# Attention and feed-forward block on one core: the value products of a unit gathered into one run, with new constants in the planner

## The chip, the cores and the metric

One NeuronCore of a Trainium2 chip runs the whole kernel. The metric is the device time of one execution in microseconds (us), lower is better. Before the change the median of three runs is 1599.75 us (1596.24 to 1602.34).

## The reference, cut to what matters

A transformer block on x of 2 x 1024 x 512 in float32: layer norm with a shift and a scale from a small vector, attention (32 query heads, 8 key heads, 64 wide, rotary positions, causal), a gated residual, a second layer norm, a feed-forward part with ternary weights (groups of 64), and a gated residual. The part that the change touches is this:

```
scores = jnp.einsum('bhqd,bhkd->bhqk', q, k) / jnp.sqrt(jnp.float32(D))
scores = jnp.where(causal[None, None], scores, jnp.finfo(x.dtype).min)
attn = jax.nn.softmax(scores, axis=-1)
out = jnp.einsum('bhqk,bhkd->bhqd', attn, v)
```

## The kernel before, in words

The kernel has four stages in time: projections of q, k and v (in the profiled execution up to about 316 us), attention (the first scores at 317 us, the last row sums end at 1050 us), the product with Wo together with the second norm (from 1039 us), and the feed-forward part (from 1232 us to the end).

**Units.** Attention is cut into 64 units: 2 batches, 8 key heads, and 4 groups of 256 queries, each for the 4 query heads of a key head. A unit of group i has 2, 4, 6 or 8 key blocks of 128 keys (nb = 2 * i + 2). The groups come in the order 2, 4, 6, 8, except in the last key head of the last batch, where it is reversed. So there are 16 rounds of four units with 20 blocks each.

**What a unit does.** Tiles are named as in the profile.

- Tops. To have a value to subtract in the softmax, TensorE first multiplies queries and keys once in a single pass, queries on the partitions: `pm`, two matmuls at a time on two 64-row halves of the array, each into a PSUM bank of its own. VectorE reduces each `pm` to a maximum per query: `mm` by a plain reduction, `junk` (followed by a read of the accumulator, `mx`) by a reduction with the causal mask. 48 such reductions belong to a round. The maxima are turned (`mt`) and go by DMA into a row (`row`).
- Scores. For each key block TensorE makes exact scores with keys on the partitions, from high and low parts, and subtracts the row of maxima: tiles `ps_`, two PSUM banks for a chain of blocks. Within a chain the next block is accumulated onto the banks of the block before, after ScalarE has read that with its exponentials (`e`, two of 128x512 for a block).
- Values. `value(j)` multiplies a block's exponentials with the values, `po`, on two 64-column halves of the array, in one PSUM bank for the whole unit. The bank is claimed by the first value task and freed when ScalarE has copied `po` out (`on`).
- Sums. GpSimd, and VectorE for block 1, add the exponentials (`acc`); TensorE sums them over the keys with ones (`pr`, four 32-column quarters). The inverse goes through DRAM and comes back as `ri`; GpSimd multiplies `on` with it.

Beside attention runs the rounding of the feed-forward weights, 48 tiles of 128x512: three ScalarE steps, one matmul (`pq`) and six VectorE steps (`ws`, `wm_`, `wr`). The first TBEFORE = 20 of them are due within attention.

**What sets the order.** Every task of attention and of what follows is added to a planner (class Plan) with an engine, a cost, a due time and what it needs. `Plan.run` keeps a modelled clock and takes tasks one by one; the order in which it takes them is the order in each engine's queue, since every engine is kept in program order. A PSUM tile (tag "#") gets the bank that is free first by the model. For TensorE the choice is in lines 129 to 133: of the tasks that can start within TURN, the one with the least due time, corrected by STICK (a bonus for the mode that the array is in), LATE (a penalty for a task that becomes ready only just then), and BOOST or DELAY for the tops, which feed VectorE, by how much VectorE work is `behind` (BOOST below FEED). A move out of mode 3 (tops and scores) is put off for a top while less than FILL is behind:

```
best = min((o for o in opts if o[0] <= start + TURN),
           key=lambda o: (o[2].due - STICK * (CLASS[o[2].mode] == CLASS[mode]) + LATE * o[1] - (o[2].feeds > 0) * (BOOST * (behind < FEED) - DELAY * (behind > ENOUGH)), o[2].n))
if mode == 3 and best[2].mode != 3 and behind < FILL:
    best = min((o for o in opts if o[0] <= start + TURN and o[2].feeds > 0), key=lambda o: (o[2].due, o[2].n), default=best)
```

The modes are ways of cutting the array: 0 whole, 1 the values, 2 the row sums, 3 tops and scores. The values of a unit become tasks of SPAN[nb] blocks each (lines 974 to 982); a value task is one uninterrupted stretch of TensorE's queue:

```
if (at + 1) % SPAN[nb] == 0:
    js = order[at + 1 - SPAN[nb]:at + 1]
    v = add("T", (SPAN[nb] * 2048 - (1024 if nb - 1 in js else 0)) / 2400 + 0.02, due + 5,
            lambda js=js: [value(x) for x in js], sum((ex[x] for x in js), []) + [kd["lv"]], order=vals[-1:],
            takes=("#",) if at == SPAN[nb] - 1 else (), mode=1)
```

The exponentials lie in 4 + 10 buffers (EB, EL), each held until its value task and the sums have read it. LEAD sets how long before a unit's first scores its tops are due (lines 868 to 892), TBEG how long before the end of attention the first 20 weight tiles begin to be due (line 1327). All operations are recorded by one helper, so the profile has one line, L39, for nearly all, and groups are told by their tiles.

Of the kernel before, what the change touches and what calls it, by code (L numbers as in the profile page):

```python
# [61 lines left out]
class Plan:  # L62
# [10 lines left out]
    def add(self, eng, cost, due, emit, after=(), order=(), takes=(), dma=0, mode=0, lane=None):  # L73
        t = Task(len(self.tasks), eng, cost, due, emit, after, order, takes, dma, int(isinstance(cost, Two)) if eng == "V" else mode, lane)
        self.tasks.append(t)
        return t
# [99 lines left out]

WARM = (12, 4)
EB, EL = 4, 10
SPAN = {2: 2, 4: 4, 6: 3, 8: 4}
HELD = 4  # L180
TBEG, TEND, PER_UNIT = 300, 20.0, 0.8
VSUM, VSIGN, LAST = 9, 1, 3
TBEFORE, TGAP, TSKIP = 20, 20.0, 25.0
LEAD, SPREAD, STICK, LATE = 15, 0.6, 9, 4
ENTER, LEAVE, LOAD, AHEAD = 0.16, 0.37, 0.1, 0.25
CLASS = (0, 1, 1, 2)
TURN, SPARE = 0.05, 1.0
FEED, BOOST, ENOUGH, DELAY, FILL = 0.3, 22, 2, 8, 3.5
QT, PACE = 6, 4

@with_exitstack
def block_kernel(ctx, tc, x, wq, wk, wv, wo, wgu, wpj, cin, wmod, cos, sin, out):
# [430 lines left out]
    def ac(n, psum=True):  # L623
        return (0.075 if psum else 0.1) + n / 1200
# [153 lines left out]
    def attention(u):  # L778
# [142 lines left out]
        def causal(j):  # L921
            q0 = 128 if j == nb - 1 else 0
            e = d["e", j][:, :, q0:q0 + 128]
            P.affine_select(out=e, in_=e, pattern=[[0, 4], [1, 128]], compare_op=ALU.is_ge, fill=0.0, base=0,
                            channel_multiplier=-1)

        def value(j):
            q0 = 128 if j == nb - 1 else 0
            if j == order[0]:
                d["po"] = otile("po").rearrange("p (a q) -> p a q", q=256)  # L930
            vv = K[(b, g // 2 * 2)]["vt"][:, j, g % 2 * 64:g % 2 * 64 + 64]
            for hp_ in range(2):
                T.matmul(d["po"][hp_ * 64:hp_ * 64 + 64, :, q0:], vv, d["e", j][:, hp_ * 2:hp_ * 2 + 2, q0:],
                         start=(j == order[0]), stop=(j == order[-1]))
# [15 lines left out]
        for at, j in enumerate(order):  # L950
# [21 lines left out]
            if j >= nb - 2:  # L972
                ex[j] = [add("P", 0.6, due - 1, lambda j=j: causal(j), es[j])]
# [5 lines that stand above are left out]
                kd["av"].append(v)  # L979
# [46 lines left out]
        for j in range(nb):  # L1026
            es[j][0].hold("eb" if late_e[u, j] else "e", vals[order.index(j) // SPAN[nb]], *([rs] if nb == 2 or j == nb - 2 else adds[j or added[0]]))
        rc = add("A", ac(256), t1_ + 5, row_copy, (rs,), order=(opened,), takes=("ls",))
# [597 lines left out]
```

## Time and profile before

| | |
|---|---|
| median of three runs | 1599.75 us |
| the profiled execution | 1598.2 us |
| its span, first to last instruction | 1596.3 us |
| TensorE (PE) busy | 1548.1 us, 97% |
| VectorE (DVE) busy | 1175.4 us, 74% |
| GpSimd (POOL) busy | 863.0 us, 54% |
| ScalarE (ACT) busy | 697.8 us, 44% |
| mean granted TensorE clock | 0.990 |

So 1.9 us lie outside the span. Two facts are needed to read the tables. Matmuls overlap in the array, so PE's busy time counts every matmul from its first to its last result, and a PE that shows 97% is not a PE at its peak: what counts is the distance between the starts of two matmuls. And PEld, the loading of weights, is issued by the same queue as PE and ahead of its matmul; a wait that is booked on PEld may or may not cost PE time.

### The profile page before, as it was taken

The numbers are of one execution on the slowest core, as the hardware profiler recorded it, in microseconds if no ns is written. First come the engines' busy times: TensorE is split into PE (matmuls) and PEld (weight loads), VectorE is DVE, ScalarE is ACT, GpSimd is POOL, SyncE is SP. The second block draws the span as 40 slices with busy tenths as digits, with TensorE's granted clock in tenths as the row PEclk, the third lists the DMA queues.
The fourth block names the chain that finished last, engine by engine and source line by source line (L and its number), as shares of the span: only waits on it lengthen the run. The fifth ranks groups of instructions, "written<-read, shape, count | busy, mean of one in ns | idle before, by whom it ended". The sixth has DMA issues, their size and how long they took to land.

```text
span 1596.3 us, 26757 instructions
## 1 busy us (share of the span) xinstructions
PE 1548.1 (97%) x9028; PEld 1068.0 (67%) x9028; DVE 1175.4 (74%) x2468; ACT 697.8 (44%) x1349; POOL 863.0 (54%) x758
## 2 busy tenths in 40 slices
PE   8899998989999999999999999999999999999998
PEld 7777887745555555555555555477788887888886
DVE  6888887778777788888878888857888674443444
ACT  3322222146555556555555656634655432222221
POOL 4364556537666765765676675713323544444343
PEclk9999999999999999999999999999999999999999
DMA  7775758775555546655646555576777833020000
GB/s 247 243 201 173 225 150 230 227 182 163 154 146 150 143 125 172 167 157 141 169 123 172 146 150 144 161 244 198 251 216 246 288 102 136 1 79 1 11 16 27
DMA packets 206592, 250.55 MB, mean 157 GB/s; under 512 B 34932, under 2 KB 144500, under 8 KB 206456
## 3 DMA queue, kind: packets, MB, share of 16 engines
q1 hardware_dynamic: 206456, 248.85, 53.0%
q8 instruction: 71, 1.16, 0.3%
q14 instruction: 65, 0.53, 0.1%
HBM read 156.24 MB, written 92.02 MB: 156 GB/s over the span
## 4 chain that ended last, share of the span: by engine, by line
PE 70%; DVE 13%; DMA 6%; issue 5%; SPq 3%; ACT 2%; POOL 1%; DVEq 0%; ACTq 0%; POOLq 0%
PE pgu L39 15%; PE po L39 13%; PE pj L39 10%; PE pfo L39 7%; PE pqk L39 6%; PE pm L39 5%; DVE junk L39 3%; SPq L39 3%; PE pr L39 2%; DVE rr L39 2%; DMA k<-ks 1%; DMA t<-qs 1%; DVE mm L39 1%; DVE ra L39 1%; DVE rd L39 1%
## 5 line engine op out<-in xcount | busy, mean ns | idle before, releaser
L39 POOL TENSOR_TENSOR acc<-acc,e 128x512 f32<-128x512 f32 x202 | 266.0, 1328 | 61.6 <-DVE acc L39 47.7
L39 PE MATMUL po<-e,vt 128*64 128x512 f32 (+1 forms) x1280 | 268.0, 557 | 4.2 <-DVE mx L39 1.6
L39 PE MATMUL pgu<-h,gu 128*128 128x512 f32 x1024 | 244.3, 391 | 0.0
L39 PEld LDWEIGHTS pgu<-h,gu 128*128 128x128 f32 x1024 | 192.0, 188 | 39.8
L39 DVE CUSTOM_DVE_ANT_0 junk<-pm,cmask,mm 128x384 bf16<-128x384 f32 (+1 forms) x256 | 174.6, 682 | 57.7 <-PE pm L39 33.2
L39 PEld LDWEIGHTS po<-e,vt 128*64 128x64 f32 x1280 | 84.0, 136 | 154.8 <-issue 123.3
L39 PE MATMUL pm<-k,t 64*128 64x384 f32 (+3 forms) x768 | 167.1, 384 | 16.1 <-DVE mx L39 6.0
L39 POOL TENSOR_SCALAR_AFFINE_SELECT e<-e 128x512 f32<-128x512 f32 x128 | 88.3, 692 | 143.6 <-ACT e L39 140.9
L39 PEld LDWEIGHTS pm<-k,t 64*128 64x128 f32 x768 | 93.5, 185 | 105.6 <-issue 31.6
L39 POOL TENSOR_TENSOR s<-hm 128x512 f32<-128x512 f32 x59 | 68.7, 1164 | 163.3 <-DVE hm L39 163.1
L39 DVE CUSTOM_DVE_ANT_0 junk<-pm,cmask 128x128 bf16<-128x128 f32 (+3 forms) x256 | 124.6, 487 | 41.4 <-PE pm L39 18.8
L39 DVE TENSOR_REDUCE mm<-pm 128x1 f32<-128x384 f32 (+2 forms) x256 | 128.3, 546 | 31.6 <-PE pm L39 31.1
L39 PE MATMUL pj<-woH,oh 128*128 128x512 f32 x512 | 142.2, 399 | 0.0
L39 POOL TENSOR_TENSOR on<-on,ri 128x512 f32<-128x512 f32 x64 | 85.5, 1337 | 66.8 <-DMA ri<-linv 62.7
L39 DVE TENSOR_TENSOR mL<-hm,mH 128x512 fp32r<-128x512 f32 x64 | 75.9, 1186 | 60.7 <-ACT mH L39 60.7
L39 DVE TENSOR_TENSOR hm<-gs,pgu 128x512 f32<-128x512 f32 x64 | 43.9, 686 | 94.3 <-PE pgu L39 89.9
L39 PEld LDWEIGHTS pj<-woH,oh 128*128 128x128 f32 x512 | 95.1, 188 | 20.9 <-issue 2.3
L39 ACT ACTIVATE mH<-hm 128x512 fp32r<-128x512 f32 x64 | 40.4, 632 | 146.1 <-PE pfo L39 133.3
L39 POOL TENSOR_TENSOR ra<-ra,rb 128x512 f32<-128x512 f32 x40 | 51.7, 1291 | 94.4 <-DVE rb L39 82.5
L39 PE MATMUL pfo<-pj,mH 128*128 128x512 f32 x256 | 100.4, 392 | 0.0
L39 PE MATMUL pfo<-pj,mL 128*128 128x512 f32 x256 | 99.7, 389 | 0.0
L39 POOL TENSOR_TENSOR sq<-sq,s 128x512 f32<-128x512 f32 x59 | 80.8, 1369 | 4.5
(1485 smaller groups left out, 3667.6 us busy)
## 6 DMA issues: line engine op xcount, KB each, us to landing
qs<-rr SPq DMA_DIRECT2D x128, 256.0 KB
t<-qs SPq DMA_DIRECT2D x64, 512.0 KB
k<-ks SPq DMA_DIRECT2D x64, 256.0 KB
ri<-linv SPq DMA_DIRECT2D x128, 128.0 KB
os<-on SPq DMA_DIRECT2D x64, 256.0 KB
ks<-rr SPq DMA_DIRECT2D x32, 256.0 KB
w<-in_wgu SPq DMA_DIRECT2D x32, 256.0 KB
gus<-wr SPq DMA_DIRECT2D x32, 256.0 KB
```

The lines of the kernel that those rows point to most:

```text
L39: ins = f(*a, **k)
```

## The change

The value tasks of the units with 6 and 8 blocks, which were two tasks of 3 and of 4 blocks, become one task of 6 and of 8 blocks. In the same edit six constants of the planner get other values.

```diff
-SPAN = {2: 2, 4: 4, 6: 3, 8: 4}
+SPAN = {2: 2, 4: 4, 6: 6, 8: 8}
...
-TBEG, TEND, PER_UNIT = 300, 20.0, 0.8
+TBEG, TEND, PER_UNIT = 330, 20.0, 0.8
...
-LEAD, SPREAD, STICK, LATE = 15, 0.6, 9, 4
+LEAD, SPREAD, STICK, LATE = 11, 0.6, 6, 1
...
-FEED, BOOST, ENOUGH, DELAY, FILL = 0.3, 22, 2, 8, 3.5
+FEED, BOOST, ENOUGH, DELAY, FILL = 0.6, 22, 2, 8, 1
```

No operation is added or taken away; what changes is the order in every engine's queue from about the end of the projections on into the feed-forward part (the last 819 rows of TensorE's queue are the same), and the PSUM banks that the tiles get.

## The prediction

> **What bounds the kernel now.** I read the page first, then the sums of the attention stretch, then its groups, its waits, and last the order in time.
>
> ```profile
> PE 1548.1 (97%) x9028; PEld 1068.0 (67%) x9028; DVE 1175.4 (74%) x2468; ACT 697.8 (44%) x1349; POOL 863.0 (54%) x758
> PEld 7777887745555555555555555477788887888886
> DVE  6888887778777788888878888857888674443444
> ```
>
> PE looks full everywhere, but from the 9th to the 26th slice (attention) weight loads fall from 7 or 8 tenths to 5 while DVE stands at 7 or 8. The stretch from 340 to 1000 us in one row, columns PE, PEld, DVE, ACT, POOL:
>
> ```profile
> 340.00:1000.00 660.00, 641.58 (x4800) 352.75 (x4798) 540.74 (x1502) 371.87 (x772) 438.49 (x397) 1.00 0.56 153
> ```
>
> DVE is idle for 660.0 - 540.7 = 119.3 us. Its groups there (busy, mean ns, idle before and what ended it):
>
> ```profile
> L39 DVE CUSTOM_DVE_ANT_0 junk<-pm,cmask,mm 128x512 bf16<-128x512 f32 (+1 forms) x242 | 165.2, 683 | 56.1 <-PE pm L39 33.2 <-PE ps__12062 L39 0.7 <-DVE mx L39 0.5
> L39 DVE TENSOR_REDUCE mm<-pm 128x1 f32<-128x384 f32 (+2 forms) x240 | 120.4, 546 | 29.1 <-PE pm L39 28.6
> L39 DVE CUSTOM_DVE_ANT_0 junk<-pm,cmask 128x384 bf16<-128x384 f32 (+3 forms) x229 | 111.9, 489 | 32.3 <-PE pm L39 12.1 <-PE ps__7004 L39 0.2
> ```
>
> Nearly all its idle time, 56.1 + 29.1 + 32.3 = 117.5 us, lies before reductions of tops: DVE waits for PE to make a `pm`. PE waits the other way round:
>
> ```profile
> PEld pm L39 <- DVE mx L39: 25.0, 55, 0.8
> PEld pm L39 <- DVE mm L39: 9.1, 28, 0.8
> ```
>
> All waits of PE and PEld for DVE here add up to 104 us. Loads run ahead, so the loss is smaller: by the starts of the matmuls, gaps over 0.15 us that DVE ended make some 42 us. So two engines feed each other through eight PSUM banks, each stands still while the other lags, and the mixing of their work sets the time. How a value run looks from both sides:
>
> ```profile
> 847.41 0.20 DVE L39 RECIPROCAL l<-l 128x8 f32<-128x8 f32 x1
> 849.16 0.62 DVE L39 CUSTOM_DVE_ANT_0 junk<-pm,cmask,mm 128x384 bf16<-128x384 f32 x1 [1.55 <-PE pm L39]
> ```
>
> ```profile
> 845.96:848.68 2.72, 2.72 (x13) 0.77 (x12) 1.50 (x6) 0.90 (x2) 2.72 (x4) 1.00 0.52 172
> 849.75:855.48 5.73, 5.73 (x30) 1.92 (x28) 5.34 (x8) 1.89 (x4) 5.04 (x4) 1.00 0.14 46
> ```
>
> The first window is a run of 12 value matmuls (3 blocks): DVE does 1.50 of 2.72 us and waits for the next `pm`. The second has 28 (two tasks that met): DVE had 5.34 of 5.73 us in its queue, sums and weight rounding among it. **A value run gives DVE nothing**; what was ready when it began decides whether DVE stands.
>
> **The change, step by step.** I built the changed kernel and compared the queues. All operations remain, so only order counts. Value runs fall from 92 to 63: before, 29 of 3.0 and 14 of 3.4 us, 31 of 2.1 and 2.6; after, 16 of 4.7 and 16 of 6.4, one per unit of 6 or 8 blocks (streaming times: a block is 0.85 us, a unit's last one half of that; the other runs are mostly units of 2 blocks).
>
> *Mode changes, -3.0.* The 28-matmul run holds 6.5 full blocks' worth, the 12-matmul run 3: (5.73 - 2.72) / 3.5 = 0.86 us a block, and 2.72 - 3 x 0.86 = 0.14 us is entry and exit; with the streaming 0.85 it is 0.17. I take 0.16, or 0.08 for one change of mode. The queue has 313 changes before and 276 after, so -37 x 0.08 = -3.0. The Trainium skill (TensorEngine Tiling (Array Packing), Key Properties) says that a change of tiling mode drains TensorE; it gives no price, and these rows do.
>
> *More turns between tops and scores, +2.1.* With the lower STICK and LATE and the higher FEED, separate stretches of tops rise from 289 to 316. In the trace a score after a top starts 0.08 us later than it streams (9.5 us over 121 such steps): 27 x 0.08 = +2.1, between 0 and twice that. So PE's own work hardly changes: -0.9.
>
> *DVE left without work, +9.5.* For each run I took the last DVE result that PE has waited for by then, and added up, with the rows' mean durations, the DVE work from there to the first reduction whose `pm` stands behind the run. More DVE cannot have left. Before, this falls short of the runs by 7 us in all, and the trace has DVE idle for 57 us in its 92 runs: 50 us, 0.54 a run, come on top because DVE is ahead of what PE forced. After, the 8-block runs have 6.1 us of cover for 6.6 us, but the 6-block runs only 2.5 for 4.8: shortfall 15 x 2.25 + 15 x 0.55 = 42 us. With 0.54 for each of 63 runs that is 76 us, or 19 us more idle DVE. What passes into the time lies between 0 (the other 62 us of DVE's idle time, in stretches of tops and scores, shrink by as much) and all 19; if DVE ran exactly at what PE forces, the whole rise of the shortfall, 42 - 7 = 35. PE's loss to DVE is now 42 us for 119 idle, 0.35 for one; DVE has less room after, so I take half of 19.
>
> *Exponentials bunched, +3.* Between the 4-block run and the 6-block run PE now streams 7.3 us with 6.9 blocks of scores (before, up to the first half: 5.9 us, 5.5 blocks). A 128x512 exponential takes 0.609 us, two a block: 6.9 x 1.22 = 8.4 us of ACT, of which up to 4 (2.4 us) can be left for the run. That just fits; other ACT work (`on` 0.597, `ls` 0.389) makes it tight. Below nothing is excluded, as ACT has the same work in fewer openings; above, 1 us in each of 15 rounds, 15. I take 0.2 a round, 3, since PE's waits for ACT in this stretch are now 16 us, mostly under running matmuls.
>
> *At nothing.* LEAD: by streaming time, the least distance between a unit's last top and the first score that needs its row is 6.5 us before, 6.3 after; the trace has one 0.5 us matmul wait for a row, so the row's trip is covered; without it each unit would pay its difference, at most some tenths. The row, sum and copy DMAs that SP issues for a unit move with it. TBEG: one weight tile fewer (20 for 21) stands before the last value run, some 4 us of DVE, done later beside the product with Wo, where PE streams without it. Buffers of `e`: 8 + 6 blocks just fill the 14; the unit after next needs the first ones when their run is past, so no wait follows unless a run is late. The last 819 rows of PE's queue are unchanged.
>
> **Sum.** -3.0 + 2.1 + 9.5 + 3 = +11.6 on 1598.2 us (span 1596.3 and 1.9 outside it): 1609.8. The median of the runs is 1.55 above the profiled execution; with that, **1611 us**. With its own uncertainties (DVE 0 to 19, ACT 0 to 6, turns 0 to 4) this case spans 1597 to 1627.
>
> Against the change speaks a page, too: the Trainium skill (Perfetto Trace Analysis, Optimization Strategy) expects gains from interleaving regimes whose busiest engine differs. Runs of values are PE's and POOL's regime (1.50 us of DVE in 2.72), tops are DVE's, and the change interleaves them less. No run shown so far measures the rule.
>
> **The rivals.**
>
> *Long runs are covered: faster.* The 28-matmul run leaves DVE idle for 0.39 us, fewer than two short ones (0.88 a run on average for the 31 of 3 blocks, 0.61 for the 43 of 4). The bank of `po` is no longer held across two tasks, so tops can stand ready. If the 32 long runs leave 0.39 each and the 31 others keep some 0.4, DVE idles 25 us instead of 57; half of these 32 us, 16, and the switches give 1598.2 - 16 - 0.9 + 1.5 = 1583. It decides if DVE has over 4 us queued when a 6-block run starts; the count allows 2.5. Against it also: that long run lived on weight rounding and sums, not on tops.
>
> *Nothing passes on: no change.* DVE fills what it lost in the runs from its 62 idle us elsewhere, ACT fits: 1598.2 - 0.9 + 1.5 = 1599. For it: PE's work is unchanged, and PE bounds most of the stretch.
>
> *All passes on: much slower.* 19 for DVE, 15 for ACT, 2.1 more turns than taken: 1599.75 - 0.9 + 36 = 1635.
>
> That the runs are not formed is excluded by the built queue.
>
> **How the numbers follow.** My forecast has 0.45, the covered runs 0.29, no change 0.16, all passing 0.10. The range takes in the rivals' times but for their outer halves: 1580 to 1634. What a measurement of this kernel can tell from no change is about 0.5%, 8 us: faster than 1592 is the first rival, 0.29 and a little, 0.30; within, the third with the low end of the forecast, 0.17; slower, 0.53.
>
> **What would show it.** In the attention stretch after: DVE idle above 119 us, its gaps before `junk` and `mm` ending on `pm` after runs of 24 value matmuls, each over 2 us; PE waiting less for DVE just after such a run and more in the tops behind it; runs costing 0.16 us beyond their blocks. If DVE is busy through 6-block runs, the cover was counted wrongly and the first rival holds; if PE's score gaps end on `e`, ACT is the bound.

## The result and the profile after

| | before | after |
|---|---|---|
| median of four runs each | 1597.99 us (1594.94 to 1602.34) | 1617.47 us (1614.92 to 1619.33) |
| profiled execution | 1598.2 us | 1617.03 us |
| its span | 1596.3 us | 1615.3 us |
| mean granted clock | 0.990 | 0.988 |

The change makes the kernel slower: after / before = 1.0123 [1.0105, 1.0141]. The forecast was 1611 us. The page of the changed kernel, its first rows (busy time and share of each engine; then weight loads and VectorE in 40 slices):

```profile
PE 1552.3 (96%) x9028; PEld 1075.5 (67%) x9028; DVE 1177.8 (73%) x2468; ACT 698.2 (43%) x1349; POOL 862.9 (53%) x758
PEld 7677786655555555555555555476787887888886
DVE  6888886778787778778878789748877775444444
```

The sums hardly differ from those of before, and the dip of PEld is the same. The difference shows in the stretch from 340 to 1000 us (columns us, PE, PEld, DVE, ACT, POOL, clock, DMA share, GB/s):

```profile
340.00:1000.00 660.00, 632.91 (x4707) 353.71 (x4703) 529.54 (x1462) 364.30 (x753) 424.88 (x384) 0.99 0.55 150
```

In the same 660 us PE now gets through 4707 matmuls instead of 4800, and DVE is idle for 130.5 us instead of 119.3. VectorE's groups in this stretch, after (busy, mean ns, idle before and what ended it):

```profile
L39 DVE CUSTOM_DVE_ANT_0 junk<-pm,cmask,mm 128x512 bf16<-128x512 f32 (+1 forms) x236 | 161.6, 685 | 77.2 <-PE pm L39 55.5 <-PE ps__8310 L39 0.3
L39 DVE TENSOR_REDUCE mm<-pm 128x1 f32<-128x384 f32 (+2 forms) x235 | 118.2, 545 | 19.6 <-PE pm L39 18.2 <-PE ps__5177 L39 0.8 <-PE ps__10103 L39 0.3
L39 DVE CUSTOM_DVE_ANT_0 junk<-pm,cmask 128x128 bf16<-128x128 f32 (+3 forms) x224 | 109.3, 488 | 32.3 <-PE pm L39 10.3 <-DVE mx L39 0.5
```

All durations are as before (685 ns against 683, 545 against 546). The idle time has moved to the first group: 77.2 us for 56.1, of which 55.5 (before 33.2) ended when a `pm` came.

**Where the 19 us are.** I cut the span at the first scores and at the end of the last row sums. Attention takes 747.1 us instead of 732.7 (+14.4), the rest after it 550.5 instead of 546.2 (+4.3), the projections ahead of it 317.8 instead of 317.4. Inside attention I let each matmul stream from its start and took what the next start comes later than that: gaps over 0.15 us by what ended them, smaller ones together.

| in attention, us | before | after | change |
|---|---|---|---|
| PE's gaps ended by VectorE | 46.2 | 72.3 | +26.1 |
| PE's gaps ended by ScalarE | 10.1 | 11.2 | +1.1 |
| ended by others, or unnamed | 14.9 | 12.3 | -2.6 |
| gaps under 0.15 us (modes, turns) | 61.9 | 54.7 | -7.2 |
| DVE idle, all of attention | 134.6 | 151.9 | +17.3 |
| DVE idle inside value runs | 56.9 | 81.0 | +24.1 |

The four kinds of gap add up to +17.4, 3 us more than attention's +14.4; this difference of the streaming model is not explained. (The prediction's "some 42" for PE's loss to VectorE was for 340 to 1000 us; 46.2 is the same measure over all of attention.)

One run of 24 value matmuls from both sides. VectorE's order in time, after (start, length, idle before it in brackets):

```profile
581.26 1.42 DVE L39 TENSOR_REDUCE mm<-pm 128x1 f32<-128x256 f32 x4
587.09 0.62 DVE L39 CUSTOM_DVE_ANT_0 junk<-pm,cmask,mm 128x384 bf16<-128x384 f32 x1 [4.41 <-PE pm L39]
```

TensorE's order in time around it:

```profile
580.91 0.52 PE L39 MATMUL pm<-k,t 64*128 64x256 f32 x3
581.74 4.94 PE L39 MATMUL po<-e,vt 128*64 128x512 f32 x24 [0.32 <-DVE mm L39]
586.62 0.44 PE L39 MATMUL pm<-k,t 64*128 64x384 f32 x2
...
588.45 0.53 PE L39 MATMUL pm<-k,t 64*128 64x384 f32 x2
589.31 0.38 PE L39 MATMUL pq<-wabs,gones 128*128 128x512 bf16 x1 [0.33 <-DVE mx L39]
```

And the window of the run:

```profile
581.74:586.62 4.88, 4.88 (x25) 1.64 (x26) 0.94 (x3) 0.63 (x2) 4.88 (x5) 1.00 0.49 149
```

Before the run PE itself waits 0.32 us for VectorE to clear a bank, so VectorE is then left with nothing but the four short reductions it has begun: 0.94 us of work for 4.88 us. It stands for 4.41 us, and 2.7 us behind the run PE waits for VectorE again. A stretch without work for the one becomes a wait of the other.

### The profile page after: what moved, and what is told of

Same layout as the page of the kernel before. It is cut to its first block, busy times and chain, and to the rows that moved or that the text cites. A ratio compares the mean times of both kernels' runs of the same rounds, so it can differ in the third digit from the quotient of the medians.

```text
span 1615.3 us, 26733 instructions
## 1 busy us (share of the span) xinstructions
PE 1552.3 (96%) x9028; PEld 1075.5 (67%) x9028; DVE 1177.8 (73%) x2468; ACT 698.2 (43%) x1349; POOL 862.9 (53%) x758
## 3 DMA queue, kind: packets, MB, share of 16 engines
q1 hardware_dynamic: 206456, 248.85, 52.3%
## 4 chain that ended last, share of the span: by engine, by line
PE 67%; DVE 14%; issue 4%; DMA 3%; ACT 1%; SPq 1%; POOL 1%; DVEq 0%; ACTq 0%; POOLq 0%
PE pgu L39 14%; PE po L39 13%; PE pj L39 10%; PE pfo L39 7%; DVE junk L39 6%; PE pqk L39 5%; PE pm L39 4%; DVE mm L39 2%; PE pr L39 2%; DVE acc L39 1%; DMA qs<-rr 1%; SPq L39 1%; PE pv L39 1%; DVE ws L39 1%; DVE rr L39 1%
## 5 line engine op out<-in xcount | busy, mean ns | idle before, releaser
L39 PE MATMUL po<-e,vt 128*64 128x512 f32 (+1 forms) x1280 | 263.4, 558 | 2.5 <-DVE mx L39 1.2
L39 PE MATMUL pm<-k,t 64*128 64x384 f32 (+3 forms) x768 | 181.6, 384 | 25.7 <-DVE mx L39 13.6
L39 PEld LDWEIGHTS pm<-k,t 64*128 64x128 f32 x768 | 101.2, 186 | 104.1 <-DVE mx L39 35.2
L39 DVE CUSTOM_DVE_ANT_0 junk<-pm,cmask 128x128 bf16<-128x128 f32 (+3 forms) x256 | 124.9, 488 | 40.5 <-PE pm L39 15.7
L39 ACT ACTIVATE on<-po 128x512 f32<-128x512 f32 x64 | 38.2, 597 | 182.9 <-POOL acc L39 68.0
L39 ACT ACTIVATE mH<-hm 128x512 fp32r<-128x512 f32 x64 | 40.4, 632 | 147.4 <-PE pfo L39 134.6
```

The source lines that it names most:

```text
L39: ins = f(*a, **k)
```

## The experiments

The table has all runs. "Rest" is from the last row sum to the end of the span. "Lost to DVE" and "to ACT" are PE's gaps as above. The ratios are to before, each with its own runs of before on the same chip.

| run | median us | ratio [95%] | attention | rest | lost to DVE | to ACT | small gaps |
|---|---|---|---|---|---|---|---|
| before | 1597.99 | | 732.7 | 546.2 | 46.2 | 10.1 | 61.9 |
| after | 1617.47 | 1.0123 [1.0105, 1.0141] | 747.1 | 550.5 | 72.3 | 11.2 | 54.7 |
| span_only | 1613.55 | 1.0106 [1.0076, 1.0135] | 746.5 | 548.1 | 62.6 | 12.8 | 55.0 |
| consts_only | 1608.87 | 1.007 [1.005, 1.009] | 729.3 | 554.5 | 44.7 | 10.8 | 60.9 |
| eight_only | 1616.06 | 1.0125 [1.0092, 1.0159] | 750.0 | 550.8 | 61.3 | 13.1 | 59.6 |
| six_only | 1617.21 | 1.013 [1.0091, 1.0168] | 749.3 | 551.2 | 52.3 | 20.9 | 59.3 |
| twos | 1611.0 | 1.0082 [1.0059, 1.0106] | 733.2 | 557.1 | 40.5 | 7.7 | 66.6 |
| control_stick | 1597.7 | 1.0013 [0.9998, 1.0028] | 728.3 | 552.2 | 38.7 | 12.5 | 62.4 |
| control_lead | 1601.59 | 1.0033 [1.002, 1.0045] | 733.5 | 547.7 | 42.1 | 12.4 | 64.2 |
| light_before | 1566.69 | 0.9823 [0.9793, 0.9853] | 700.9 | 545.5 | 10.1 | 18.7 | 61.7 |
| light_after | 1570.83 | 0.9838 [0.9817, 0.986] | 698.2 | 550.5 | 14.2 | 18.5 | 55.3 |
| light_eight | 1586.0 | 0.9932 [0.9905, 0.9958] | 716.6 | 550.7 | 12.1 | 25.4 | 59.0 |
| cost_before | 1603.01 | 1.0038 [1.0024, 1.0053] | 727.1 | 554.8 | 27.6 | 19.3 | 64.7 |
| cost_after | 1601.14 | 1.003 [1.0018, 1.0041] | 722.6 | 555.9 | 26.4 | 25.3 | 61.7 |

### Is VectorE the cause? The same queues with lighter reductions

The theory: the long runs cost because VectorE, which has no work in them, has no room to catch up. Rivals: ScalarE's bunched exponentials, and that any other order costs about as much. In both kernels each reduction of a top reads only the first half of its columns (so the subtracted maximum is taken over half of the keys); all queues keep their order.

```diff
-V.tensor_tensor_reduce(junk[:, :w], pm[:, :w], cmask[:, 512 - w:], 1.0, low, ALU.add, ALU.max, dst)
+V.tensor_tensor_reduce(junk[:, :w // 2], pm[:, :w // 2], cmask[:, 512 - w:512 - w // 2], 1.0, low, ALU.add, ALU.max, dst)
...
-V.tensor_reduce(dst, pm[:, :w], AX.X, ALU.max)
+V.tensor_reduce(dst, pm[:, :w // 2], AX.X, ALU.max)
```

Of light_before, the edit on before, this was expected:

> The kernel before, queues and banks unchanged, but each reduction of a top on VectorE reads only the first half of its columns, so the subtracted maximum is that of half the keys. By 60 to 270 ns a reduction, 768 of them, VectorE loses some 130 us of work. DVE theory: a large part of the 46 us that PE loses to VectorE in attention goes, 20 to 40 us faster, 1557 to 1577. Rival, PE or ScalarE bounds attention and VectorE's waits are covered: within 8 us of before.

Of light_after, the edit on after:

> The changed kernel with the same halved reductions (only the first half of the keys enters the subtracted maximum). DVE theory: with VectorE out of the way the difference between the two kernels, now 19 us, shrinks to what is left outside VectorE, between -3 (mode changes) and +6 (clock, the stage with Wo) against the light kernel before. Rival, ScalarE bunched or some other engine: the difference stays at 15 us or more.

The difference of 19.5 us falls to 4.1 (1566.69 against 1570.83), and all of that lies in the rest (+5.0); attention is now 2.7 us shorter with the long runs. The 340 to 1000 us windows, light_before's first:

```profile
340.00:1000.00 660.00, 653.19 (x5020) 361.86 (x5022) 438.90 (x1548) 391.24 (x816) 464.62 (x416) 1.00 0.58 160
```

and light_after's:

```profile
340.00:1000.00 660.00, 652.80 (x5005) 368.91 (x5002) 425.65 (x1544) 390.30 (x814) 461.83 (x415) 1.00 0.58 160
```

PE gets through nearly the same number of matmuls in both (5020 and 5005), with ACT busier than in either full kernel (391 us against 372 and 364). In light_after VectorE's idle time in the value runs is 121 us, more than anywhere else, and it hardly costs anything: PE's loss to VectorE is 4.1 us above light_before's, and attention is shorter. So idle time of VectorE is harmful only where it leads to PE's waits for it, and those are 14.2 us here and 72.3 in after. ScalarE's rival falls for this change: its work is the same in the light kernels, and PE's loss to it is the same in both (18.7 and 18.5).

### Is it any other order? Two controls

Each changes one constant of before a little, which reorders the queues and leaves SPAN as it is.

```diff
-LEAD, SPREAD, STICK, LATE = 15, 0.6, 9, 4
+LEAD, SPREAD, STICK, LATE = 15, 0.6, 8.5, 4
```

> The kernel before with the planner's STICK at 8.5 instead of 9: run lengths as before, only a reshuffled order (shortfall 6 us against 7, 312 mode changes against 313). DVE theory: within 4 us of before. Rival, lottery: the constants of before are a lucky draw and any reshuffle costs as much as the long runs did, +12 us or more.

```diff
-LEAD, SPREAD, STICK, LATE = 15, 0.6, 9, 4
+LEAD, SPREAD, STICK, LATE = 14, 0.6, 9, 4
```

> The kernel before with LEAD at 14 instead of 15: again run lengths as before (shortfall 10 us against 7, the same 313 mode changes). DVE theory: 0 to +5 us. Rival, lottery: +12 us or more.

Measured +2 (not told from none) and +5 us by the ratios. Attention went by -4.4 and +0.8 us, the rest by +6.0 and +1.5. So a small change of the order alone does not cost 19 us; but it can cost several in the rest, a point that comes back below. Whether a larger one can is another matter: see eight_only and light_eight.

### The parts of the change

Value runs alone, with the constants of before:

```diff
-SPAN = {2: 2, 4: 4, 6: 3, 8: 4}
+SPAN = {2: 2, 4: 4, 6: 6, 8: 8}
```

> The value runs of the change (6 and 8 blocks in one) with the planner constants of before. DVE theory (the loss is VectorE left without work in long value runs): counted from the built order as in the prediction, the cover falls short of the runs by 26 us in all, against 7 before and 42 in the changed kernel; at 0.55 us of time for each, and 48 mode changes fewer at 0.08 us, about +7 us on before, so 1605, with VectorE idle for 2 to 3 us in a 6-block run. Rival, the constants are the loss: 0 to 4 us faster than before, 1594 to 1598. Rival, exponentials bunched on ScalarE by the long runs: nearly the whole loss, +15 us or more, with score gaps ending on exponentials.

The constants alone, with the value tasks of before:

```diff
-TBEG, TEND, PER_UNIT = 300, 20.0, 0.8
+TBEG, TEND, PER_UNIT = 330, 20.0, 0.8
...
-LEAD, SPREAD, STICK, LATE = 15, 0.6, 9, 4
+LEAD, SPREAD, STICK, LATE = 11, 0.6, 6, 1
...
-FEED, BOOST, ENOUGH, DELAY, FILL = 0.3, 22, 2, 8, 3.5
+FEED, BOOST, ENOUGH, DELAY, FILL = 0.6, 22, 2, 8, 1
```

> The planner constants of the change with the value runs of before (3 and 4 blocks). DVE theory: shortfall 14 us against 7, 17 mode changes and 40 stretches of tops more than before: +3.9 + 1.4 + 3.2, about +8 us at most, and far less than the whole loss if the turns are cheap. Rival, the constants are the loss: +15 us or more. Rival, ScalarE bunched: about 0, since the scores are not bunched.

The runs alone give +17 us, where +7 was expected, nearly all of it in attention (+13.8). The constants alone give some +11 (1.007). Their trace is of the fastest of the eight runs, 1602.66 us, and so accounts for some 5 of the 11: attention is 3.4 us shorter, the rest 8.3 longer. The median's other 6 us have no trace, but the recorded clocks tell of most of them: the eight runs have a median granted clock of 0.988 where the traced one has 0.991, which over 1600 us is an estimated 5 us more of lost clock, if PE sets the time throughout. The two parts do not add up (17 + 11 against 19). The prediction had counted how much VectorE work must be left when each run begins; by that count, before falls 7 us short of the runs, span_only 26, after 42. DVE's idle time in the runs follows it (56.9, 71.2, 81.0), but the time of span_only does not: by the ratios it is 3 us from after's where it should be halfway. Nor does PE's loss: consts_only has 69.1 us of idle VectorE in its value runs, 12.2 more than before, and loses 44.7 us to VectorE, 1.5 less.

Only the 8-block units in one run, with the constants of before:

```diff
-SPAN = {2: 2, 4: 4, 6: 3, 8: 4}
+SPAN = {2: 2, 4: 4, 6: 3, 8: 8}
```

> Constants of before; only the units of 8 blocks are multiplied in one run, those of 6 stay at 3 and 3. DVE theory: shortfall 16 us, 23 mode changes fewer: (16 - 7) x 0.55 - 1.8 = +3 us. Rival, long runs as such cost by bunching exponentials: the 8-block units hold most of it, +8 us or more. Rival, constants: -2 us.

Only the 6-block units in one run, with the constants of before:

```diff
-SPAN = {2: 2, 4: 4, 6: 3, 8: 4}
+SPAN = {2: 2, 4: 4, 6: 6, 8: 4}
```

> Constants of before; only the units of 6 blocks are multiplied in one run, those of 8 stay at 4 and 4. DVE theory: the 6-block runs are the ones that VectorE cannot cover, shortfall 22 us, 23 mode changes fewer: (22 - 7) x 0.55 - 1.8 = +6 us, more than the 8-block runs cost. Rival, bunching of exponentials: less than the 8-block runs cost. Rival, constants: -2 us.

Both came out at +20 and +21 us, as much as both parts together. With shortfalls of 16 and 22 us they should have been far below. In eight_only PE loses 15.1 us more to VectorE and 3.0 to ScalarE; in six_only 6.1 and 10.8: there PE's loss to ScalarE is the larger part.

The same edit on eight_only (reductions of half their width) was to show if VectorE makes the 20 us there as it does in after:

```diff
-SPAN = {2: 2, 4: 4, 6: 3, 8: 4}
+SPAN = {2: 2, 4: 4, 6: 3, 8: 8}
...
-V.tensor_reduce(dst, pm[:, :w], AX.X, ALU.max)
+V.tensor_reduce(dst, pm[:, :w // 2], AX.X, ALU.max)
```

(and the masked reduction as in light_before)

> The kernel with only the 8-block runs joined, which lost 20 us where the count had 3, now with the halved reductions on VectorE (only half the keys enter the subtracted maximum). DVE theory, the count being too small but VectorE the cause: within -2 to +7 us of the light kernel before (1567), the upper end being the stage with Wo. Rival, another mechanism (GpSimd's sums, exponentials, stalls on the inverse): it keeps 12 us or more, 1579.

It doesn't: light_eight is 19.3 us above light_before (17 by the ratios), about as much as eight_only is above before. Of attention's +15.7 us, only 2.0 is lost to VectorE; ScalarE has 6.7, DMA 3.2, GpSimd 2.2, unnamed 4.3, small gaps -2.7. One of these waits, in ScalarE's order in time of light_eight:

```profile
678.06 0.62 ACT L39 ACTIVATE e<-ps__7957 128x512 f32<-128x512 f32 x1
680.98 0.38 ACT L39 ACTIVATE ls<-pr 128x256 f32<-128x256 f32 x1 [2.29 <-DMA l<-ls]
```

and what TensorE has of it:

```profile
681.41 0.33 PE L39 MATMUL pm<-k,t 64*128 64x128 f32 x2 [1.50 <-ACT ls L39]
```

The copy of the row sums, `ls`, has one buffer, which the DMA `l<-ls` must have read; in ScalarE's queue it stands ahead of exponentials that could run, and PE stands with them. There are three such waits of 1.5 to 1.9 us, and one of 2.5 us for a transfer (`t<-qs`). They make 7.7 us; the rest of the 19 is spread, 5.2 of it behind attention. What causes this in the 8-block runs alone, and why after, which contains them, does not suffer from it with light reductions, stays open. So VectorE is shown as the cause for after as a whole, not for every order with long runs. Six_only was not tried with light reductions.

Shorter runs than before, as the reverse:

```diff
-SPAN = {2: 2, 4: 4, 6: 3, 8: 4}
+SPAN = {2: 2, 4: 4, 6: 2, 8: 2}
```

> Constants of before, the runs made shorter: units of 6 and 8 blocks in twos. Shortfall 3 us against 7, but 365 mode changes against 313. DVE theory with 0.08 us a change: -2 + 4 = +2 us, 1599. If mode changes cost more than the rows of before show, up to 0.3 us each as the planner has it: +14 us.

The time is +13 us (1.0082), for neither of the reasons given. Attention is as long as before (+0.5 us): PE loses 5.7 us less to VectorE and 2.4 less to ScalarE, and pays 4.7 us in small gaps for 52 more changes of mode, 0.09 us each. The rest has +10.9, with two waits for `wabs`, 4.4 and 3.4 us, beside the product with Wo (they end at 1081.5 and 1126.5 us). In each of them the clock fell to half for 6.8 us. With that, the clock lost in the rest is 7.4 us instead of 1.5, so up to 5.9 of the 10.9 us are the clock's.

### Long runs, with VectorE's work priced as the trace has it

If the harm comes from VectorE being late behind the runs, the planner must have counted on it being on time. In before's trace the starts of masked reductions with their accumulator read follow one another by 0.77 us at 384 columns where VectorE is busy (0.71 for those that do not start from `mm`); the planner has 0.544 (0.484). Plain reductions of 384 columns follow by 0.47, and it has 0.469. So only the masked ones are too cheap, by some 0.23 us. The edit gives them 0.2 us more and changes nothing else:

```diff
-r = add("V", dv(w) + ((0.075 if c else 0.015) if tag == "mx" else 0.0), due + 0.01 * n_, ...
+r = add("V", dv(w) + ((0.28 if c else 0.21) if tag == "mx" else 0.0), due + 0.01 * n_, ...
```

On after:

> The changed kernel, long runs and its constants kept, but the planner is told the cost that the trace shows for a masked reduction (0.28 or 0.21 us above the plain one instead of 0.075 or 0.015), so it puts more VectorE work ahead of the runs: the counted shortfall falls from 42 to 17 us, mode changes 281 against 276. DVE theory: long runs cost only by their missing cover, so (42 - 17) x 0.55 = 14 us less than the changed kernel, about 1604, and 6-block runs leave VectorE idle for about 1 us instead of 3.2. Rival, long runs cost as such: 1613 or more.

On before:

> The kernel before with the same corrected cost of masked reductions in the planner: shortfall 3 us against 7, 311 mode changes against 313. DVE theory: (3 - 7) x 0.55 = 2 us faster, 1595, give or take the 5 us that a reshuffled order moves in the stage with Wo. If it wins 8 us or more it beats both kernels.

Cost_after has the same long runs as after (17 of 24 matmuls, 16 of 32) and takes 1601.14 us, 16 less (15 by the ratios). Its attention is 722.6 us, 24.5 us shorter than after's and 10.1 shorter than before's. PE's loss to VectorE is 26.4 us, little over a third of after's; its loss to ScalarE rises to 25.3. The 340 to 1000 us window:

```profile
340.00:1000.00 660.00, 648.21 (x4811) 358.23 (x4813) 538.88 (x1499) 372.79 (x772) 442.90 (x396) 1.00 0.55 155
```

and one run of 24 there, the window and then VectorE's order in time:

```profile
569.86:574.73 4.87, 4.87 (x25) 1.63 (x25) 3.84 (x10) 1.05 (x2) 4.79 (x5) 1.00 0.71 219
```

```profile
572.86 1.26 DVE L39 TENSOR_TENSOR wm__6421<-ws,wabs 128x512 bf16<-128x512 bf16 x1
575.26 0.69 DVE L39 CUSTOM_DVE_ANT_0 junk<-pm,cmask 128x512 bf16<-128x512 f32 x1 [1.15 <-PE pm L39]
```

VectorE does 3.84 us of work in this run, where after's had 0.94, and stands for 1.15 us. This run is one of the better ones: over all 17, VectorE is idle for 2.27 us each, where after has 3.16 and about 1 was expected. By the count of the queues the shortfall is 17 us instead of 42. So PE's loss fell by 45.9 us while VectorE's idle time in all value runs fell only from 81.0 to 65.6. Cost_before shows that over half of the gain belongs to the price and not to the runs: its attention is 727.1, 5.6 us below before's. With equal prices the long runs have 4.5 us less of attention, by one trace of each (both the fastest of ten, 1599.22 and 1598.0 us). In the whole time this does not arrive: the rest is 9.7 us longer than before's in cost_after and 8.6 in cost_before (there up to 4.4 of them are the clock, which loses 5.9 us instead of 1.5), 1601.14 and 1603.01 us stand beside 1597.2 of before, and their intervals overlap. No kernel with the whole computation beats before; one with cost_after's attention and before's rest was not tried.

## Why the prediction was right, and where its sizes were off

The direction, the place and the mechanism were right: VectorE without work in the 24-matmul runs, and PE's waits for it behind them. The sizes were not: PE's loss to VectorE came out at nearly three times its term, and by luck mode changes saved more than was put and took back part of that error.

**DVE left without work.** For the 6-block runs the prediction had 2.25 + 0.54 = 2.8 us of idle DVE each and for the 8-block runs 0.55 + 0.54 = 1.1; the trace has 3.16 (17 runs) and 1.17 (16 runs). In all 76 us were predicted, 81.0 measured. This count held for after.

**"Half passes on" failed**, and is the main error. The step took half of 19 us, because PE's loss was 0.35 us for one of idle DVE before. Measured: DVE's idle in the runs +24.1 us, PE's loss to it +26.1. So as much as all of it passed on, by the totals. An average of before says nothing of the next microsecond, and neither does the idle time by itself: the light pair has idle time that costs little while VectorE has room (+27 us of it in the runs, +4.1 us lost), consts_only has 12.2 us more than before and loses 1.5 less, cost_after 8.7 more and loses 19.8 less. That after pays in full because VectorE has no room behind its runs fits the light pair; the room itself was not measured. The third rival's first term, 19 for DVE, was the better one. Some of the 26 us, at most 5.1, is the clock: three windows of half clock stand in after's attention, 17.0 us long together, and one of 6.8 us in before's; half of each is lost, so the difference is 8.5 - 3.4 = 5.1 us.

**Mode changes and turns, -3.0 + 2.1 = -0.9:** small gaps fell by 7.2 us. Each part was mis-sized: 37 changes fewer gave 7.2 us in after, 0.19 each if the turns cost nothing; 48 fewer in span_only gave 6.9 (0.14 each); 52 more in twos cost 4.7 (0.09). The 0.08 is at the low end, and of the +2.1 for turns there is no sign. The long run itself was priced rightly: the 24-matmul window above is 4.88 us, which is 5.5 blocks of 0.86 and 0.15 more, against 0.16 predicted.

**Exponentials bunched, +3:** ScalarE's gaps rose by 1.1 us. The mechanism is real in other orders (six_only +10.8, cost_after +15.2), so its range up to 15 was not too wide.

**At nothing:** LEAD and TBEG were put at no cost, which leaves the rest after attention at before's 546 us. It took 4.3 us more. The first products with Wo in after, TensorE's order in time:

```profile
1090.81 0.39 PE L39 MATMUL pq<-wabs,gones 128*128 128x512 bf16 x1
1092.21 0.50 PE L39 MATMUL pj<-woH,oh 128*128 128x512 f32 x1 [1.01 <-ACT woH L39]
1093.25 0.96 PE L39 MATMUL pj<-woH,oh 128*128 128x512 f32 x3 [0.54 <-ACT woH L39]
```

Before had no wait for `woH` here, a part of Wo that ScalarE makes. These two cost some 2 us against streaming starts; the other 2 us were not traced to a line. The rest moved in nearly every run: with an order other than before's it was 1.5 to 10.9 us longer in every run with full reductions, and in light_before, whose order is before's, 0.7 shorter. Before's rest is at the low end of all orders seen, and the prediction had put no price on losing that.

**The sum.** Forecast +11.6 on the profiled execution, measured +18.8: +26.1 for 9.5, -7.2 for -0.9, +1.1 for 3, +4.3 for 0, with the others' -2.6 and 3 us that the model of streaming leaves over. (The upper end of the prediction's own case adds up to 1626 us, not 1627.)

**The rivals.** Covered runs would have needed 0.39 us of idle DVE for a long run; the 24-matmul runs have 3.16. "Nothing passes on" falls with PE's +26.1. And by cost_after the long runs are not bad in themselves: what cost in after is runs without VectorE work ready, which follows from where the tops stand in the queue. (In light_eight long runs cost 17 to 19 us by other waits, so this is no account of every order.) The Trainium skill (Perfetto Trace Analysis, Optimization Strategy) speaks for interleaving regimes of different engines; span_only, at +17 us, agrees, and cost_after, at the same length of runs, shows that a coarser interleaving with work laid up ahead of it costs attention nothing (722.6 us).

**What would show it.** DVE idle above 119 us: 130.5. Gaps over 2 us that end on `pm` behind runs of 24: in 14 of the 17, of 3.0 to 4.4 us; the other three have none. PE waiting more in the tops behind the runs: by the starts of matmuls, yes; by the rows of waits it is hard to see. In after, columns us in total, times, longest:

```profile
PEld pm L39 <- DVE mx L39: 29.4, 59, 1.4
...
PEld pm L39 <- DVE mm L39: 8.3, 24, 1.2
```

These were 25.0 and 9.1, so +3.6 us for a loss that rose by 26. The longest wait, 1.4 and 1.2 for 0.8 each, tells more: loads run ahead of PE, and not every wait of theirs costs it time.

## What to carry to other kernels

Where two engines feed each other through a few buffers, a longer uninterrupted run on one can cost what the other lacks in work at its start: count that from the queue, and let the range reach to all of it. Here it came back in full in one order and hardly at all in others, so the count tells where to look and is not a price. Before blaming a coarser grain, check the scheduler's prices against the spacing of starts in the trace: with one price put right, the same long runs cost some 15 us less. And a reordering is not over where it ends: look at what comes after it, where before's order may hold a few microseconds that any other order loses.

## What was not expected of the hardware

The clock of TensorE was halved in a place where PE never stood for long. After, 4 us windows from 352 us (the clock is the figure after POOL's):

```profile
352.00:356.00 4.00, 2.63 (x23) 1.12 (x18) 3.22 (x12) 1.46 (x4) 0.00 (x0) 0.96 0.62 188
356.00:360.00 4.00, 3.68 (x11) 1.92 (x13) 3.62 (x13) 1.10 (x2) 0.00 (x0) 0.50 0.63 173
360.00:364.00 4.00, 4.00 (x27) 3.02 (x25) 3.43 (x11) 2.43 (x5) 1.96 (x2) 0.68 0.42 117
```

and before, the same times:

```profile
352.00:356.00 4.00, 2.73 (x20) 1.26 (x20) 3.57 (x11) 0.60 (x1) 2.10 (x2) 1.00 0.36 99
356.00:360.00 4.00, 3.20 (x25) 1.66 (x19) 3.69 (x14) 2.68 (x5) 0.00 (x0) 1.00 0.44 139
```

From 355.7 us on the clock stands at 0.50 for 6.8 us in after. PE had three waits for VectorE ahead of it, 0.33, 0.47 and 0.46 us, and was busy for 2.63 of 4 us; before had gaps of 0.46, 0.41 and 0.40 us and 2.73 us busy, and kept the full clock. All such stretches in attention were 3.4 or 6.8 us long. So a series of short waits can go before a slower clock, and two nearly equal series differ; what decides was not settled.

The Trainium skill (TensorE: Matmul & The Clock Gate, What's actually happening) puts half the clock after a window of some 3.4 us in which the array is idle. No gap here came near that, so for this place the rule does not foretell what the rows show; the 3.4 us agree with the lengths. Where PE stood longer, in the waits of 4.4 and 3.4 us in twos, the clock did fall to half, for 6.8 us each.
